# Attention values in fewer, longer bursts, and the room in SBUF that this takes

## The chip, the cores and the metric

The kernel runs on one core of one Trainium2 chip. The metric is the device time of one execution in microseconds (us). Before the change the median of three runs is 1562.35 us (1560.28 to 1562.48).

The core's engines work side by side, each through its own instructions in order: TensorE (PE in the profile, its weight loads PEld), VectorE (DVE), ScalarE (ACT), GpSimd (POOL), and SyncE (SP), which here issues nearly all DMAs. An instruction waits for semaphores that others raise; what stands behind it on the same engine waits with it.

## The reference

Eight batches of 1024 tokens with 256 features go through one gated block. Cut to what matters:

```python
xn = layernorm(x)                                  # no learned scale
q, k, v = split(xn @ W_attn + b_attn, 3)           # 16 heads of 16
q, k = rope(q), rope(k)                            # see below
att = softmax(where(causal, q @ k.T / sqrt(16), -inf))
s = (att @ v) @ W_proj + b_proj
h = silu(xn @ (w_gate / 127).T) * (xn @ (w_up / 127).T)   # 768 hidden, integer weights
g = silu(h @ (w_down / 127).T)
out = x + s * g
```

(The angles of rope depend on the head here and not on the token, so the kernel folds them into the weights once.)

## The kernel before

**Groups and halves.** The 16 heads of a batch form four groups of four, so there are 32 groups in all. A group works through its queries in two halves of 512. For half 0 there are four blocks of 128 keys, for half 1 eight: twelve *steps* n = 0 to 11 (`weight_steps`, L551). A step on the diagonal needs fewer queries: n = 0 to 3 have 512, 384, 256 and 128 columns, n = 4 to 7 have 512, and n = 8 to 11 again 512, 384, 256 and 128.

**One step.** `weights` (L554) makes the exponentials for one pair of heads: PE multiplies k by q into a PSUM tile `pw` (two of them, L564), ACT takes the exponential into a tile `e` in SBUF (L571), and on the diagonal POOL zeroes what lies above it (`affine_select`, L578). A step has two pairs, hence two `e` tiles. They come from the pool `pe` of six tiles, all of 2 x 512 columns whatever the step needs, used in turn. `values` (L592) multiplies v by these exponentials and adds up in the PSUM tile `av` (L600): four matmuls for the four heads, each with 32 columns of weights out of `v_sb`, side by side in the array; in fp32 each leaves two rows in the profile. v has a column of ones behind each head's 16, which makes the softmax's sum. After the last step of a half ACT copies `av` (L610), and `finish` (L613) transposes it on PE (`py`, L618) and divides on DVE.

**When values are added.** `attention` (L662) appends each finished step to `waiting`. As soon as three steps wait, `add_values(2)` (L694) does the oldest two: a *burst* of eight matmuls. The newest step always stays behind. The bursts come at the ends of steps n = 0, 2, 4, 6, 8 and 10. What `values` returns at the end of a half goes to `endings` and is called in the second pair of the next step (L683).

**The softmax's maxima.** They belong to the next group: while one group makes its weights, PE also multiplies q by k for the next group into `pm` (three PSUM tiles, L506), and DVE reduces each to row maxima (`top_far` L515, `top` L517). Their split high and low parts go through `shift_queries` (L539: transpose on PE, copy to `rows` on ACT, two DMAs on SP) into two extra rows of `q_st`, so the matmul of the weights subtracts them.

**Everything else** (projections, feed-forward, output) is cut into pieces in one long list, `chain`. `slot` (L822) is called after each bank of weights and each batch of maxima, and runs pieces so that PE's estimated work is spread evenly over a batch. The pieces use two PSUM tiles ("fill"). DVE's part of a piece is put off in `later` and issued by the next `flush`. The chain of a batch holds its feed-forward, the last batch's output and the next batch's q, k and v. The next batch's v comes last, while group 3 of the present batch runs.

**Projection of q and k** (`project_qk`, L230). PE makes `pqk` from two pieces; ACT writes `high`, a copy rounded to the matmul's reduced precision (L248), DVE writes `low`, the rest (L251), and SP sends both to DRAM (L256). `load` (L479) fetches a group's q and k from there, four DMAs each. `high` and `low` come from pool `p2`, which holds two tiles of each tag, while `p1` holds one. A tile that is used again waits until the DMA out of it has landed.

**Projection of v** (`project_v`, L263). Two token tiles at a time go to `pv`; DVE adds the bias on the way into `v_sb` (L278). There are two full `v_sb`, used by batches in turn.

**The opening.** Up to about 41 us the first batch is normalized, q and k for groups 0 and 1 are made by a Batch object called `opening`, and the weights are prepared. Then `forward` runs the maxima of group 0 with nothing to lie beside (L794): one chain piece for every two units, and among them the loads of group 1, `shift_queries(0)` for group 0 and the four remaining q/k projections of batch 0. The first weights follow.

Of the kernel before, what the change touches and what calls it, by code (L numbers as in the profile page):

```python
# [9 lines left out]
F32 = mybir.dt.float32  # L10
F32R = mybir.dt.float32r
# [3 lines left out]
ALU = mybir.AluOpType  # L15
AX = mybir.AxisListType

P = 128
HEADS = 16
HD = 16  # L20
SLOT = 32
# [14 lines left out]
def gated_block_kernel(ctx: ExitStack, tc: tile.TileContext, x, wqk, bqk, wv, bv, wp, bp, wg, wu, wd, rope, out):  # L36
# [139 lines left out]
    most = const.tile([P, 4], F32, name="most")  # L176
    flag = const.tile([1, 1], I32, name="flag")

    vs = [const.tile([P, NT, HEADS * VS + SLOT - VS], F32, name=f"v_sb_{i}") for i in range(2)]

# [11 lines left out]
        for j in which:  # L192
            engine.memset(stacks[i][j][half][PARTS:, :, :].bitcast(F32), (0.0, -1.0)[j])

    def set_ones(engine, i):
        whole = vs[i][:, :, : HEADS * VS].rearrange("p t (h s) -> p t h s", s=VS)
        engine.memset(whole[:, :, :, HD], 1.0)
        engine.memset(vs[i][:, :, HEADS * VS :], 0.0)

    p1 = ctx.enter_context(tc.tile_pool(name="p1", bufs=1))  # L200
    p2 = ctx.enter_context(tc.tile_pool(name="p2", bufs=2))
    pe = ctx.enter_context(tc.tile_pool(name="pe", bufs=6))


    QU = S // 4
# [2 lines left out]
    class Batch:  # L208
        def __init__(self, b, exact):
            self.b = b  # L210


            self.exact = exact
            self.hs = {}
# [15 lines left out]
        def project_qk(self, n, which, half, c):  # L230
            b = self.b
            i = which * (QK // 2 // P) + n
            if c == 0:
                self.pt = fill_tile("pqk")
            pt = self.pt
            nc.tensor.matmul(  # L236
                pt,
                wqk_sb[:, c, ts(i, P)],
                xnT[:, c, ts(half, HALF)],
                start=(c == 0),  # L240
                stop=(c == CC - 1),
            )
# [5 lines left out]
            nc.scalar.activation(high, pt, AF.Identity, bias=bqk_sb[:, i : i + 1])  # L248

            def rest():  # L250
                nc.vector.scalar_tensor_tensor(  # L251
                    low, pt, bqk_sb[:, i : i + 1], high.bitcast(F32), ALU.add, ALU.subtract
                )
                self.projected.add((n, which, half))
                for part, t in enumerate((high, low)):
                    nc.sync.dma_start(  # L256
                        out=qks[b % 2][which, part, ts(n, P // HD), :, ts(half, HALF)].rearrange("h d s -> (h d) s"),
                        in_=t.bitcast(F32),
                    )

            later.append(rest)

        def project_v(self, t):  # L263
            b = self.b
            if t % 2 == 0:
                self.pt = fill_tile("pv")
            pt = self.pt.rearrange("p (t d) -> p t d", t=2)
            for c in range(CC):
                nc.tensor.matmul(  # L269
                    pt[:, t % 2, :],  # L270
                    xnT[:, c, ts(t, P)],
                    wv_sb[:, c, :],
                    start=(c == 0),
                    stop=(c == CC - 1),
                )
            if t % 2:
                later.append(
                    lambda: nc.vector.tensor_tensor(  # L278
                        vs[b % 2][:, t - 1 : t + 1, : HEADS * VS].rearrange("p t (h s) -> p t h s", s=VS)[:, :, :, :HD],
                        pt.rearrange("p t (h d) -> p t h d", d=HD),  # L280
                        bv_sb.rearrange("p (h d) -> p h d", d=HD)[:, None, :, :].to_broadcast([P, 2, HEADS, HD]),
                        ALU.add,
                    )
                )

        def project_in(self):

# [180 lines left out]
    class Group:  # L468
# [85 lines left out]
        def weights(self, half, kb, pair):  # L554

            lo = max(0, kb * P - half * HALF)
            n = HALF - lo
            e = pe.tile([P, 2, HALF], F32, tag="e", name=f"e_{self.name}_{half}_{kb}_{pair}")

            def bank(first, count):  # L560
                pw = ps_pw.tile([P, HALF], F32, tag="pw", name=f"pw_{self.name}_{half}_{kb}_{pair}_{first}")
                for i in range(count):
                    head = 2 * pair + first + i
                    nc.tensor.matmul(  # L564
                        pw[:, ts(i, n)],
                        self.k_st[kb // QT][:, head, ts(kb % QT, P)],
                        self.q_st[half][:, head, lo:],
                        start=True,
                        stop=True,
                    )  # L570
                nc.scalar.activation(  # L571
                    e[:, first : first + count, lo:],
                    pw[:, : count * n].rearrange("p (a n) -> p a n", n=n),
                    AF.Exp,
                )
                if first + count == 2 and kb * P >= half * HALF:

                    nc.gpsimd.affine_select(  # L578
                        out=e[:, :, lo : lo + P],
                        in_=e[:, :, lo : lo + P],  # L580
                        pattern=[[0, 2], [1, P]],
                        compare_op=ALU.is_ge,
                        fill=0.0,
                        base=0,
                        channel_multiplier=-1,
                    )

            if 2 * n <= HALF:
                return e, [lambda: bank(0, 2), None]
            return e, [lambda: bank(0, 1), lambda: bank(1, 1)]  # L590

        def values(self, half, kb, es):  # L592
# [3 lines left out]
            if kb == 0:  # L596
                self.av = ps_av.tile([P, HALF], F32, tag="av", name=f"av_{self.name}_{half}")
            for j in range(4):
                at = (4 * self.g + j) * VS
                nc.tensor.matmul(  # L600
                    self.av[ts(j, SLOT), lo:],
                    vs[self.batch.b % 2][:, kb, at : at + SLOT],
                    es[j // 2][:, j % 2, lo:],
                    start=(kb == 0),
                    stop=(kb == last),
                )
# [20 lines left out]
            self.batch.complete[half] += 1  # L627

    STEPS = 3 * QT

    waiting, endings = [], []

# [29 lines left out]
    def attention(groups, at, plan, slot, vector):  # L662
# [5 lines left out]
        for n, (half, kb) in enumerate(group.weight_steps()):  # L668
            es = []
            for pair in range(2):  # L670
                e, banks = group.weights(half, kb, pair)
                es.append(e)
                for second, bank in enumerate(banks):
# [180 lines left out]
    with tc.tile_pool(name="setup", bufs=1) as sp:  # L854
# [21 lines left out]
        for i in range(2):  # L876
            set_ones(nc.gpsimd, i)

# [120 lines left out]
```

## Time and profile before

| what | value |
|---|---|
| median of the runs | 1562.35 us |
| profiled execution | 1562.15 us |
| its span, first to last instruction | 1560.4 us |
| granted TensorE clock over the span | 0.99 |
| `av` matmuls, L600 | 3072 rows, 290.8 us busy |
| `e`, L571 on ACT | 1280, 678.2 us busy |
| `high`, L248 on ACT | 64, 0.69 us each |
| bias add of v, L278 on DVE | 32, 0.69 us each |

The profile is of one execution and gives each instruction's start, length and releaser. Starts on PE are firm, while ends of matmuls are modelled and overlap, so PE's time is read from one start to the next. A granted clock of 1 is full speed. "Idle before, released by" names what an engine waited for; "issue" means nothing that the profile shows.

### The profile page before, as it was taken

To read this page: it belongs to the slowest core of one execution; us is meant where nothing else is said; L and a number is where in the kernel's file an instruction comes from. 1 tells how busy PE (TensorE), PEld (TensorE's weight loads), DVE (VectorE), ACT (ScalarE), POOL (GpSimd) and SP (SyncE) were. 2 spreads that over 40 slices of the span, in tenths; PEclk is the share of its full clock that TensorE was granted. 3 is DMA by queue.
4 is the path that set the end of the run, shared out by engine and by line. 5 is a ranking of instruction groups with operands and counts; after the bars stand their busy time and mean duration, and the time that the engine had idled before them with its cause. 6 is when DMAs were issued, how large, how long until landed. Compare 5 with 4: busy or idle time off the path is not lost.

```text
span 1560.4 us, 29514 instructions
## 1 busy us (share of the span) xinstructions
PE 1505.3 (96%) x9793; PEld 1058.2 (68%) x9793; DVE 1090.7 (70%) x3294; ACT 958.6 (61%) x2076; POOL 732.4 (47%) x1435
## 2 busy tenths in 40 slices
PE   4899999999999999999999999999999999999997
PEld 2577667776677766776667766777667776666664
DVE  8876776767767677776677766776776767767642
ACT  2266665676657666566655766667665766656664
POOL 4354443554436444464435734365343644434353
PEclk9899999999999999999999999999999999999999
DMA  7812544434554254543345344444455415445301
GB/s 186 185 29 42 109 104 63 96 54 104 102 103 68 49 110 96 102 76 69 91 81 112 60 96 96 74 97 63 96 110 94 78 36 123 88 70 83 49 15 44
DMA packets 86082, 132.86 MB, mean 85 GB/s; under 512 B 13856, under 2 KB 33824, under 8 KB 85920
## 3 DMA queue, kind: packets, MB, share of 16 engines
q1 hardware_dynamic: 85632, 130.60, 42.9%
q8 instruction: 80, 1.31, 0.4%
q14 instruction: 82, 0.67, 0.2%
q10 hardware_dynamic: 288, 0.27, 0.1%
HBM read 87.83 MB, written 41.94 MB: 83 GB/s over the span
## 4 chain that ended last, share of the span: by engine, by line
PE 85%; DVE 6%; ACT 2%; DMA 1%; POOL 1%; issue 1%; SPq 0%; ACTq 0%; DVEq 0%; POOLq 0%
PE pw L564 20%; PE av L600 17%; PE pm L506 16%; PE ph L327 10%; PE pqk L236 6%; PE pd L381 6%; PE pv L269 3%; PE po L434 3%; DVE top_far L515 2%; PE py L618 2%; DVE trash L517 1%; ACT e L571 1%; PE pyt L419 1%; DVE st L104 1%; PE pxt L224 1%
## 5 line engine op out<-in xcount | busy, mean ns | idle before, releaser
L571 ACT ACTIVATE e<-pw 128x512 f32<-128x512 f32 (+2 forms) x1280 | 678.2, 558 | 418.2 <-PE pw L564 393.5
L517 DVE CUSTOM_DVE_ANT_0 trash<-pm,mask_q 128x128 bf16<-128x128 f32 (+3 forms) x1024 | 500.6, 489 | 314.9 <-PE pm L506 276.7
L564 PE MATMUL pw<-q_st,k_st 67*128 67x512 f32 (+3 forms) x1536 | 548.2, 390 | 8.7 <-ACT e L571 5.4
L506 PE MATMUL pm<-k_st,q_st 65*128 65x512 f32 (+3 forms) x1536 | 529.3, 383 | 5.7 <-DMA qk<-high 1.7
L564 PEld LDWEIGHTS pw<-q_st,k_st 67*128 67x128 f32 x1536 | 282.0, 189 | 204.0 <-issue 92.9
L578 POOL TENSOR_SCALAR_AFFINE_SELECT e<-e 128x256 f32<-128x256 f32 x512 | 206.2, 408 | 412.0 <-ACT e L571 410.6
L515 DVE TENSOR_REDUCE top_far<-pm 128x1 f32<-128x512 f32 x512 | 336.7, 683 | 57.4 <-PE pm L506 56.7
L506 PEld LDWEIGHTS pm<-k_st,q_st 65*128 65x128 f32 x1536 | 279.4, 191 | 68.8 <-DVE top L517 17.0
L600 PE MATMUL av<-e,v_sb 128*32 128x512 f32 (+3 forms) x3072 | 290.8, 496 | 0.3 <-POOL e L578 0.3
L358 POOL TENSOR_TENSOR th<-th,ups 128x256 f32<-128x256 f32 x192 | 140.5, 732 | 232.7 <-DVE th L354 227.5
L600 PEld LDWEIGHTS av<-e,v_sb 128*32 128x32 f32 x3072 | 80.8, 109 | 133.0 <-issue 100.1
L362 POOL TENSOR_TENSOR h_low<-th,h_high 128x256 fp32r<-128x256 f32 x192 | 140.6, 732 | 15.4
L236 PE MATMUL pqk<-xnT,wqk_sb 128*128 128x512 f32 x256 | 133.7, 607 | 0.0
L327 PE MATMUL ph<-xnT_high,wg_sb 128*128 128x256 f32 x384 | 100.7, 284 | 0.0
L381 PE MATMUL pd<-wd_sb,h_high 128*128 128x256 f32 x384 | 98.0, 284 | 2.8 <-POOL h_high L361 2.8
L327 PE MATMUL ph<-xnT_high,wu_sb 128*128 128x256 f32 x384 | 100.5, 283 | 0.0
L327 PE MATMUL ph<-xnT_low,wu_sb 128*128 128x256 f32 x384 | 99.7, 282 | 0.0
L339 ACT ACTIVATE th<-ph 128x256 f32<-128x256 f32 x192 | 73.7, 384 | 42.2 <-PE ph L327 36.5
L327 PE MATMUL ph<-xnT_low,wg_sb 128*128 128x256 f32 x384 | 99.6, 282 | 0.0
L381 PE MATMUL pd<-wd_sb,h_low 128*128 128x256 f32 x384 | 97.2, 282 | 1.3 <-POOL h_low L362 1.3
L354 DVE SCALAR_TENSOR_TENSOR th<-th,ph 128x256 f32<-128x256 f32 x192 | 79.5, 414 | 18.6 <-ACT ups L343 17.1
L517 DVE DVE_READ_ACCUMULATOR2_ANT top<- 128x1 f32 x1024 | 84.6, 83 | 0.0
(93 smaller groups left out, 1668.2 us busy)
## 6 DMA issues: line engine op xcount, KB each, us to landing
q_st<-qk SPq DMA_DIRECT2D x256, 128.0 KB, 4.0
k_st<-qk SPq DMA_DIRECT2D x256, 128.0 KB, 5.2
qk<-high SPq DMA_DIRECT2D x64, 256.0 KB, 2.6
qk<-low SPq DMA_DIRECT2D x64, 256.0 KB, 2.8
xs<-in_x SPq DMA_DIRECT2D x16, 512.0 KB, 8.0
res<-in_x SPq DMA_DIRECT2D x32, 256.0 KB, 4.8
out<-res SPq DMA_DIRECT2D x32, 256.0 KB, 2.6
q_st<-rows SPq DMA_DIRECT2D x128, 8.0 KB, 1.9
```

The costliest lines, as they stand in the source:

```text
L236: nc.tensor.matmul(pt, wqk_sb[:, c, ts(i, P)], xnT[:, c, ts(half, HALF)], start=(c == 0), stop=(c == CC - 1),)
L327: nc.tensor.matmul(pt, self.weights[up][:, c, ts(hc, P)], part[:, c, ts(quarter, QU)], start=(c == 0 and i == 0), stop=(c == CC - 1 and i ...
L358: nc.gpsimd.tensor_tensor(h, th, ups, ALU.mult)
L362: nc.gpsimd.tensor_tensor(low, th, high.bitcast(F32), ALU.subtract)
L381: nc.tensor.matmul(pt, h[:, ts(i, P)], self.weights[2][:, hc, :], start=(hc == 0 and n == 0), stop=(hc == HC - 1 and n == len(hs) - 1),)
L506: nc.tensor.matmul(pm[:, ts(i, n)], self.q_st[half][:SHIFT, head, at], self.k_st[keys][:SHIFT, head, :n], start=True, stop=True,)
L515: nc.vector.tensor_reduce(self.top_far[:, head, qt - QT : qt - QT + 1], pm, AX.X, ALU.max)
L517: nc.vector.tensor_tensor_reduce(trash[:, :n], pm[:, ts(i, n)], mask_q[:, HALF - n :], 1.0, MASKED, ALU.add, ALU.max, self.top[:, head, qt ...
L564: nc.tensor.matmul(pw[:, ts(i, n)], self.k_st[kb // QT][:, head, ts(kb % QT, P)], self.q_st[half][:, head, lo:], start=True, stop=True,)
L571: nc.scalar.activation(e[:, first : first + count, lo:], pw[:, : count * n].rearrange("p (a n) -> p a n", n=n), AF.Exp,)
L578: nc.gpsimd.affine_select(out=e[:, :, lo : lo + P], in_=e[:, :, lo : lo + P], pattern=[[0, 2], [1, P]], compare_op=ALU.is_ge, fill=0.0, ba ...
L600: nc.tensor.matmul(self.av[ts(j, SLOT), lo:], vs[self.batch.b % 2][:, kb, at : at + SLOT], es[j // 2][:, j % 2, lo:], start=(kb == 0), sto ...
```

## The change

- **Bursts.** `add_values` no longer follows a count of three. It is called in step n = 0, 4 and 7 of each group (`BEHIND`), between the two pairs, and does all that waits: at n=0 the last group's steps 7 to 11 (five), at n=4 steps 0 to 3 (four), at n=7 steps 4 to 6 (three). `endings` are called in the first pair of a step instead of the second.
- **Weights' room.** `pe` has seven tiles instead of six. Steps of 256 and 128 columns use narrow tiles of their own from `p2` instead, two of each width.
- **v.** Columns of groups 0 to 2 are held once (`v_most`), those of group 3 twice (`v_last`, batches in turn). The bias add of v becomes two instructions.
- **High and low.** `project_qk` takes them from `p1`, one tile of each, instead of two. The `opening` takes both out of one weights' tile.

```diff
-    vs = [const.tile([P, NT, HEADS * VS + SLOT - VS], F32, name=f"v_sb_{i}") for i in range(2)]
+    LAST = HEADS - 4
+    v_most = const.tile([P, NT, LAST * VS + SLOT - VS], F32, name="v_most")
+    v_last = [const.tile([P, NT, 4 * VS + SLOT - VS], F32, name=f"v_last_{i}") for i in range(2)]
...
-    def set_ones(engine, i):
-        whole = vs[i][:, :, : HEADS * VS].rearrange("p t (h s) -> p t h s", s=VS)
-        engine.memset(whole[:, :, :, HD], 1.0)
-        engine.memset(vs[i][:, :, HEADS * VS :], 0.0)
+    def set_ones(engine):
+        for v_sb, heads in ((v_most, LAST), (v_last[0], 4), (v_last[1], 4)):
+            whole = v_sb[:, :, : heads * VS].rearrange("p t (h s) -> p t h s", s=VS)
+            engine.memset(whole[:, :, :, HD], 1.0)
+            engine.memset(v_sb[:, :, heads * VS :], 0.0)
...
-    pe = ctx.enter_context(tc.tile_pool(name="pe", bufs=6))
+    pe = ctx.enter_context(tc.tile_pool(name="pe", bufs=7))
...
-            high, low = (
-                p2.tile([P, HALF], F32R, tag=part, name=f"{part}_{b}_{i}_{half}") for part in ("high", "low")
-            )
+            if self.parts_room:
+                room = self.parts_room.tile([P, 2, HALF], F32, tag="e", name=f"parts_{b}_{i}_{half}").bitcast(F32R)
+                high, low = room[:, 0], room[:, 1]
+            else:
+                high, low = (
+                    p1.tile([P, HALF], F32R, tag=part, name=f"{part}_{b}_{i}_{half}") for part in ("high", "low")
+                )
...
-                later.append(
-                    lambda: nc.vector.tensor_tensor(
-                        vs[b % 2][:, t - 1 : t + 1, : HEADS * VS].rearrange("p t (h s) -> p t h s", s=VS)[:, :, :, :HD],
...
+                def rest():
+                    for v_sb, first, heads in ((v_most, 0, LAST), (v_last[b % 2], LAST, 4)):
+                        of = slice(first * HD, (first + heads) * HD)
+                        nc.vector.tensor_tensor(
+                            v_sb[:, t - 1 : t + 1, : heads * VS].rearrange("p t (h s) -> p t h s", s=VS)[:, :, :, :HD],
...
-            e = pe.tile([P, 2, HALF], F32, tag="e", name=f"e_{self.name}_{half}_{kb}_{pair}")
+            name = f"e_{self.name}_{half}_{kb}_{pair}"
+            if 2 * n > HALF:
+                e = pe.tile([P, 2, HALF], F32, tag="e", name=name)[:, :, lo:]
+            else:
+                e = p2.tile([P, 2, n], F32, tag=f"e_{n}", name=name)
...
-                at = (4 * self.g + j) * VS
+                head = 4 * self.g + j
+                v_sb, at = (v_most, head) if head < LAST else (v_last[self.batch.b % 2], head - LAST)
                 nc.tensor.matmul(
                     self.av[ts(j, SLOT), lo:],
-                    vs[self.batch.b % 2][:, kb, at : at + SLOT],
-                    es[j // 2][:, j % 2, lo:],
+                    v_sb[:, kb, at * VS : at * VS + SLOT],
+                    es[j // 2][:, j % 2, :],
...
+    BEHIND = (0, QT, 2 * QT - 1)
...
-                    if pair == 1 and second and endings:
+                    if pair == 0 and second and endings:
                         endings.pop(0)()
...
                 if vector:
                     vector.pop(0)()
+                if pair == 0 and n in BEHIND:
+                    add_values(len(waiting))
             waiting.append((group, half, kb, es))
-            if len(waiting) == 3:
-                add_values(2)
...
         opening = Batch(0, None)
+        opening.parts_room = pe
```

More of the change, by code (lines that the diff above doesn't have):

```diff
@@ L213, in __init__ @@
             self.exact = exact
+            self.parts_room = None
             self.hs = {}
@@ L276, in project_v @@
             if t % 2:
-                later.append(
-                    lambda: nc.vector.tensor_tensor(
-                        vs[b % 2][:, t - 1 : t + 1, : HEADS * VS].rearrange("p t (h s) -> p t h s", s=VS)[:, :, :, :HD],
[L280 to L284, printed above, removed]
+                def rest():
[3 more added lines that the diff above has]
+                            v_sb[:, t - 1 : t + 1, : heads * VS].rearrange("p t (h s) -> p t h s", s=VS)[:, :, :, :HD],
+                            pt[:, :, of].rearrange("p t (h d) -> p t h d", d=HD),
+                            bv_sb[:, of].rearrange("p (h d) -> p h d", d=HD)[:, None].to_broadcast([P, 2, heads, HD]),
+                            ALU.add,
+                        )
+                later.append(rest)
         def project_in(self):
@@ L571, in bank @@
                 nc.scalar.activation(
-                    e[:, first : first + count, lo:],
+                    e[:, first : first + count, :],
                     pw[:, : count * n].rearrange("p (a n) -> p a n", n=n),
@@ L578, in bank @@
                     nc.gpsimd.affine_select(
-                        out=e[:, :, lo : lo + P],
-                        in_=e[:, :, lo : lo + P],
+                        out=e[:, :, :P],
+                        in_=e[:, :, :P],
                         pattern=[[0, 2], [1, P]],
@@ L875, in gated_block_kernel @@
         set_rows(nc.gpsimd, 0, 1, [1])
-        for i in range(2):
-            set_ones(nc.gpsimd, i)
+        set_ones(nc.gpsimd)
         def turn(src, dst, n, even, odd):
```

## The prediction

> **What bounds the kernel now.** I read the page's engine table and its 40 slices first, then its chain. PE is busy 96% of the span, the slices show it at 9 from second to last but one, and the chain runs on PE for 85%. So PE's order of work sets the time between about 74 us (the first weights) and the last group, and what PE loses between its instructions counts in full there.
>
> ```profile
> PE 1505.3 (96%) x9793; PEld 1058.2 (68%) x9793; DVE 1090.7 (70%) x3294; ACT 958.6 (61%) x2076; POOL 732.4 (47%) x1435
> PE   4899999999999999999999999999999999999997
> PE 85%; DVE 6%; ACT 2%; DMA 1%; POOL 1%; issue 1%; SPq 0%; ACTq 0%; DVEq 0%; POOLq 0%
> ```
>
> Busy PE is not PE at its best. The list of waits has PE's weight load idle before `av`, released by nothing but "issue", far more than any other wait of PE:
>
> ```profile
> PEld av L600 <- issue: 100.1, 336, 0.8
> PEld pw L564 <- ACT e L571: 69.9, 211, 1.0
> PEld pm L506 <- DVE top L517: 17.0, 54, 0.7
> ```
>
> The timeline of PE in the middle of the kernel shows what this costs in PE's time. The columns are start, length, engine and line; lengths overlap, so I read differences of starts.
>
> ```profile
> 715.53 0.34 PE L506 MATMUL pm<-k_st,q_st 65*128 65x384 f32 x1
> 715.80 1.92 PE L600 MATMUL av<-e,v_sb 128*32 128x512 f32 x16
> 717.65 0.44 PE L564 MATMUL pw<-q_st,k_st 67*128 67x384 f32 x1
> 717.93 0.34 PE L506 MATMUL pm<-k_st,q_st 65*128 65x384 f32 x1
> ...
> 718.83 0.34 PE L564 MATMUL pw<-q_st,k_st 67*128 67x384 f32 x1
> 719.01 0.34 PE L506 MATMUL pm<-k_st,q_st 65*128 65x384 f32 x1
> 719.18 0.34 PE L564 MATMUL pw<-q_st,k_st 67*128 67x384 f32 x1
> ...
> 723.99 1.71 PE L600 MATMUL av<-e,v_sb 128*32 128x512 f32 x16
> 725.63 0.44 PE L564 MATMUL pw<-q_st,k_st 67*128 67x128 f32 x2
> ```
>
> A 384-wide `pm` or `pw` takes 0.18 us to the next start (719.01 to 719.18). The last one before a burst of values takes 0.27 (715.53 to 715.80): 0.09 lost on entering. The first `pw` after it takes 0.28 (717.65 to 717.93): 0.10 lost on leaving. Ahead of `pw` of 128 columns that is 0.05. The burst itself: two steps of 512 columns take 1.85 us, 512 and 384 take 1.64, and 256 and 128 (another place of the trace) 0.79. So 640 columns make 1.06 us, 1.66 ns each, and 0.15 us is left over that doesn't grow with columns. Inside, four waves (two a step) start 0.45, 0.43 and 0.43 us apart and reach the next `pw` after 0.54, at 512 columns; 0.24, 0.22, 0.11 and 0.22 at 256 and 128. Only the first and the last wave take longer than their columns. One burst thus costs 0.34 us beyond its columns, 0.29 before a narrow `pw`. Over all 192 bursts the starts repeat to within 0.01 us in their medians.
>
> **The bursts: 192 become 96.** Before, a group has six bursts of two steps, two of them ahead of narrow `pw`: 4 x 0.34 + 2 x 0.29 = 1.94 us. Now it has three, of four steps (n=4), three (n=7) and five (n=0 of the next group), all ahead of a 512-wide `pw`: 3 x 0.34 = 1.02. The 1536 matmuls and their columns stay. Saved 0.92 x 32 = **29 us**, all on PE's path. [...] But inner waves go exactly with their columns (0.43, 0.22, 0.11), so loads hide there, and the loss is one of a burst's ends. I go by the trace. Ends: 27 to 30 us.
>
> **Room for weights.** With seven wide tiles in turn, tile k waits for tile k-7. Counting through a group (16 wide tiles), every such tile has been freed by an earlier burst, or by the burst directly ahead on PE (second pair of n=0 and of n=7), which precedes the pair's own `pw` anyway. Narrow tiles of n=2, 3 are freed at n=4, those of n=10, 11 at n=0. No wait of ACT is added: 0. The last step's `affine_select` on POOL (0.41) now has half a step less of lead, but comes last in a burst of 2.1 to 3 us: 0.
>
> **v in three tiles.** The add of 512 elements (0.69) becomes 384 and 128. By DVE rows of 512 (0.69) and 256 (0.42) elements those are 0.55 and 0.29: +0.15, 32 times, 5 us of DVE. 28 lie under DVE's 30% of idle time; two in the opening's DVE-bound stretch cost 0.3, two before it at most 0.3: **0.6 us**; all 5 if that cover were gone. v's pieces of the next batch come after its last q/k pieces, well into group 3, while group 2's last values come at n=0 of group 3: the single tile makes no wait. Two more memsets (0.25 each) lie under POOL's 3.5 us wait for `raw`. The opening's high and low in weight tiles: ACT waited for no landing there before, so 0.
>
> **high and low once instead of twice.** Now each `high` (L248) waits for the landing of the one before it. In steady work a landing comes before the next `high` or `low` in batches 1 to 7, mostly by 3 us or more and at the least by 0.1, and up to n=4 bursts shift both alike; only one in batch 0 falls short, by 0.65. I take **1 us** (0 to 7: one 1 us miss per batch). In the opening it is otherwise:
>
> ```profile
> 47.09 0.69 ACT L248 ACTIVATE high<-pqk,bqk_sb 128x512 fp32r<-128x512 f32 x1 [4.05 <-PE pqk L236]
> 49.89 0.69 ACT L248 ACTIVATE high<-pqk,bqk_sb 128x512 fp32r<-128x512 f32 x1 [2.12 <-DMA k_st<-qk]
> 54.16 0.69 ACT L248 ACTIVATE high<-pqk,bqk_sb 128x512 fp32r<-128x512 f32 x1 [3.58 <-DMA qk<-high]
> 56.61 0.69 ACT L248 ACTIVATE high<-pqk,bqk_sb 128x512 fp32r<-128x512 f32 x1 [1.76 <-PE pqk L236]
> ...
> 51.42 0.75 DVE L251 SCALAR_TENSOR_TENSOR low<-pqk,bqk_sb,high 128x512 fp32r<-128x512 f32 x1
> 58.55 0.74 DVE L251 SCALAR_TENSOR_TENSOR low<-pqk,bqk_sb,high 128x512 fp32r<-128x512 f32 x1
> ```
>
> The first landing is at 54.05 (it held the third `high` there). Now it holds the second, until 54.8. DVE has its `low` next at 51.42, and behind that the maxima, which hold PE's three `pm` tiles: DVE, idle nowhere from 48 to 75, loses 3.4 us. The second part lands by about 57, in time for the third. That third one's issue on SP stands behind eight loads of q and k, which now start near 56. In mid-kernel (405 us) eight such loads with a `high` behind them took 10.9 us from the first issue to `high`'s landing, so it lands near 66.9, the fourth `high` ends at 67.6, and DVE's fourth `low`, due at 58.55 + 3.4, waits 5.7 us more. Together 9.1 on DVE, with `rows` (ACT) and PE's next `pm` queued behind. PE reached its first `pw` at 73.2 and sat 0.9 us for the rows' landing; the rows now land near 76, so that wait goes: **+8.5 us** (3 if DVE makes up the second wait, 10 if loads crowd).
>
> **What longer stretches cost.** A burst lets ACT and DVE catch up. Summed over PE's starts, time over the usual start-to-start is 6% of PE's time in the first us after a burst and 9 to 14% in the five after it, not rising towards the end. With 96 fewer first microseconds, 96 x 0.05 = **4.5 us** more stalls (-2 to 12). In the last group about 3.5 us of values move behind its steps 8 to 10, where ACT is near its limit: **0.5** (0 to 2). `finish` follows its burst by one step, as before, so its 0.44 us of `py` and DVE's 0.68 move without a wait.
>
> **Sum**, against the profiled execution (1562.15 us: span 1560.4 and 1.75 around it; the median of the runs is 0.2 above it): 1562.15 - 29 + 8.5 + 0.6 + 1 + 4.5 + 0.5 = 1548.3, so **1548**. With half of each term's distance to its ends added up, this case alone spans 1541 to 1556.
>
> **Rivals.**
> *Starved engines (slower).* At a burst DVE has at most three `pm` tiles, 2.1 us of work. Bursts up to 1.85 us leave it none idle; those of 2.1, 2.6 and 3.0 leave it 1.4 us a group. DVE has 32.5 us of work per group of 46.4; outside bursts that is (32.5 - 8.6)/37.8 = 63% now and (32.5 - 6.3)/37.5 = 70% then. If stalls go as load/(1-load), they grow by 37%; those above 0.14 us sum to 83 us, so +31 instead of +4.5: 1575. It decides from +18 us, 0.6 us a group. For it: `pw` has but two tiles, and burst-free stretches grow from 6 us to 11 to 15. Against: the stall share above doesn't rise with the time since a burst.
> *The opening hides the single buffer.* If the third part's landing isn't late, only the first 3.4 us or nothing is lost: 1540 to 1543. For it: landings vary from 2.0 to 7.8 us. Against: DVE has no idle time there.
> *The loss goes with steps, not bursts*[...]: no gain, 1577. Against it stand the inner waves, which show no loss at the step from one to the next.
>
> **Chances.** The sum 0.56; opening hidden 0.18; partly starved (5 to 18 us more, 1553 to 1562) 0.11; starved 0.11; loss by steps 0.04. About 0.2% (3 us) is what a measurement of this kernel can tell from no change. Faster: 0.56 + 0.18 + most of partly starved 0.09 = 0.83; the same 0.05; slower 0.12. The range for 8 in 10 takes in the hidden opening and partial starving: 1538 to 1562.
>
> **What would show it.** Right: 96 bursts; the weight load's idle before `av` near half of 100 us; groups about 45.6 us instead of 46.4; the first `pw` near 82 instead of 74 us, behind two waits of `high` for a landing. Wrong: a first `pw` at 74 to 78 (opening hidden), or more idle time of PE's loads behind `e` (69.9) and `top` (17.0), by over 20 us (starved), or more ns per column in long bursts.

## The result and the profile after

The changed kernel takes 1579.86 us (median of five runs, 1577.53 to 1580.85), where the kernel before takes 1562.35. The ratio is 1.0109, with a 95% interval of 1.0094 to 1.0124: 1.1% slower. The forecast was 1548, with a range of 1538 to 1562, so both the time and its sign were wrong.

The profiled execution took 1580.84 us with a span of 1579.1, 18.7 us more span than before. The lines of the page that answer to those shown of before, and the granted clock beneath them (40 slices of 39.5 us):

```profile
PE 1506.5 (95%) x9793; PEld 1078.9 (68%) x9793; DVE 1092.0 (69%) x3326; ACT 954.0 (60%) x2076; POOL 731.2 (46%) x1437
PE   4789999999999999999999999999999999999997
PEclk9799999989999999989999999998999999999999
PE 80%; ACT 6%; POOL 4%; DVE 3%; issue 2%; DMA 0%; SPq 0%; POOLq 0%; DVEq 0%; ACTq 0%
```

PE is still busy in 95% of the span and still bounds the kernel. Two things are new. The clock row has an 8 in three slices in mid-kernel, where before had none. And the chain of the last end gives 4% to POOL and 6% to ACT, against 1% and 2% before. The waits of PE and of its feeders (engine, operation, line, released by: total us, count, longest):

```profile
PEld av L617 <- issue: 125.9, 440, 0.7
PEld pw L580 <- ACT e L587: 73.8, 224, 0.8
PEld pm L518 <- DVE top L529: 24.8, 70, 2.6
ACT high L256 <- DMA qk<-high: 15.9, 3, 9.0
PE pm L518 <- ACT yT L437: 10.7, 6, 1.8
ACT xs L135 <- POOL newton L126: 8.7, 6, 1.5
```

The last three lines lead to where the time went. ACT's `high` waits three times for a landing, all in the opening. PE waits six times for `yT`, a copy on ACT, and ACT waits six times for `newton` on POOL: once in each of batches 1 to 6. The first line did not fall although the bursts were halved; that is taken up below.

**The opening.** ACT's timeline (start, length, line, idle before and its releaser):

```profile
53.14 0.69 ACT L256 ACTIVATE high<-pqk,bqk_sb 128x512 fp32r<-128x512 f32 x1 [4.74 <-DMA qk<-high]
55.99 0.69 ACT L256 ACTIVATE high<-pqk,bqk_sb 128x512 fp32r<-128x512 f32 x1 [2.16 <-DMA qk<-high]
65.68 0.69 ACT L256 ACTIVATE high<-pqk,bqk_sb 128x512 fp32r<-128x512 f32 x1 [9.00 <-DMA qk<-high]
```

Each `high` now waits for the one before to land, as forecast, and the first `pw` comes at 81.92 us instead of 74.25: 7.7 us of the 18.7.

**The steps.** From the first `pw` to the last row of PE the time went from 1478.6 to 1489.6 us, 11.0 more, where the forecast had 22 less. Groups 4, 8, ... 24, the first of each later batch, take 48.4 to 49.8 us and three of their successors about 50, where the others of these batches take 45.4 to 45.9 (before: 46.7 or 46.8 for the first of a batch, 46.2 to 46.8 for the rest). The place is the same in all six, at step n = 11. Here it is in group 4, PE's timeline first:

```profile
313.00 0.40 PE L518 MATMUL pm<-k_st,q_st 65*128 65x512 f32 x1
313.24 0.33 PE L580 MATMUL pw<-q_st,k_st 67*128 67x128 f32 x2
315.35 0.50 PE L518 MATMUL pm<-k_st,q_st 65*128 65x512 f32 x1 [1.78 <-ACT yT L437]
```

ACT's at the same time:

```profile
311.91 0.38 ACT L355 ACTIVATE ups<-ph 128x256 f32<-128x256 f32 x1
313.74 0.60 ACT L135 ACTIVATE xs<-xs,newton,rstd 128x256 f32<-128x256 f32 x1 [1.45 <-POOL newton L126]
314.24 0.58 ACT L587 ACTIVATE e<-pw 128x512 f32<-128x512 f32 x1
314.72 0.58 ACT L437 COPY yT<-pyt 128x512 f32<-128x512 f32 x1
```

And POOL's:

```profile
309.18 1.29 POOL L460 TENSOR_TENSOR o<-o,gate 128x512 f32<-128x512 f32 x1 [1.02 <-DVE o L457]
310.55 1.30 POOL L461 TENSOR_TENSOR res<-res,o 128x512 f32<-128x512 f32 x1
...
313.47 0.23 POOL L126 TENSOR_SCALAR newton<-newton 128x8 f32<-128x8 f32 x1
```

`xs` is the first scaling of the next batch's x; its bias is `newton`, the last of the short operations by which POOL works out mean and variance. They stand behind two operations of 1.3 us. ACT comes to `xs` 1.45 us too early, and behind `xs` stand the exponentials and the copy `yT`, whose PSUM tile `pyt` holds one of the three `pm` tiles. PE stands still for 1.78 us. In the kernel before the same pair just fitted (timeline, POOL then ACT):

```profile
303.86 0.23 POOL L126 TENSOR_SCALAR newton<-newton 128x8 f32<-128x8 f32 x1
304.52 0.60 ACT L135 ACTIVATE xs<-xs,newton,rstd 128x256 f32<-128x256 f32 x1
```

POOL was done at 304.09, 0.4 us before ACT asked. What lay in this stretch was the burst that used to end n = 8. PE before, then PE after, from the same piece `po` on (rows in between left out):

```profile
296.96 1.03 PE L434 MATMUL po<-wp_sb,yT 128*128 128x256 f32 x4
...
298.09 1.92 PE L600 MATMUL av<-e,v_sb 128*32 128x512 f32 x16
...
304.20 0.60 PE L419 MATMUL pyt<-ident,y 128*128 128x128 f32 x4
```

```profile
306.69 1.03 PE L446 MATMUL po<-wp_sb,yT 128*128 128x256 f32 x4
...
311.85 0.60 PE L431 MATMUL pyt<-ident,y 128*128 128x128 f32 x4
```

Counted from this `po`, POOL has `newton` after 7.1 us before and 7.0 after, so it lost nothing. ACT comes for it after 7.6 us before and 5.6 after: 2 us sooner, which is the burst of 1.85 us with its ends. (The burst that used to end n = 10 begins at 305.68, behind this place. It hid no wait of ACT, but it was work for PE while ACT waits; run 7 shows what that is worth.)

The stall has a second cost. Windows of this trace (us; busy time of PE, PEld, DVE, ACT, POOL with counts; granted clock; share and GB/s of DMA) from group 4's steps over the stall and on:

```profile
268.90:316.90 48.00, 45.62 (x314) 34.10 (x312) 35.12 (x115) 28.42 (x62) 24.87 (x54) 1.00 0.53 100
316.90:327.10 10.20, 10.20 (x48) 5.29 (x50) 4.01 (x15) 3.16 (x7) 7.49 (x13) 0.50 0.74 104
327.10:367.80 40.70, 40.46 (x296) 32.05 (x288) 28.49 (x84) 28.96 (x67) 17.32 (x35) 1.00 0.19 34
```

About 1.6 us after the stall PE gets half its clock for 10.2 us, and does 48 matmul rows in them. The same 10.2 us follow in groups 12 and 20, from 692.4 and 1067.9 us; in the other three batches nothing follows (the last section says which stalls these are). With half clock the two groups that share these 10.2 us take 49.1 and 50.0 us (4 and 5), 49.6 and 49.5 (12 and 13), 49.8 and 49.3 (20 and 21); without it 48.4 and 45.8 (8 and 9). That is 4.9 us more for each such pair of groups.

### The profile page after: what moved, and what is told of

Read it like the earlier page. It is cut to its first block, busy times and chain, and to the rows that moved or that the text cites. A ratio compares the mean times of both kernels' runs of the same rounds, so it can differ in the third digit from the quotient of the medians.

```text
span 1579.1 us, 29394 instructions
## 1 busy us (share of the span) xinstructions
PE 1506.5 (95%) x9793; PEld 1078.9 (68%) x9793; DVE 1092.0 (69%) x3326; ACT 954.0 (60%) x2076; POOL 731.2 (46%) x1437
## 4 chain that ended last, share of the span: by engine, by line
PE 80%; ACT 6%; POOL 4%; DVE 3%; issue 2%; DMA 0%; SPq 0%; POOLq 0%; DVEq 0%; ACTq 0%
PE pw L580 18%; PE av L617 17%; PE pm L518 16%; PE ph L339 9%; PE pqk L240 6%; PE pd L393 5%; PE po L446 3%; ACT e L587 3%; PE pv L277 3%; PE py L635 2%; DVE trash L529 1%; DVE top_far L527 1%; POOL th L370 1%; POOL e L594 1%; ACT high L256 1%
## 5 line engine op out<-in xcount | busy, mean ns | idle before, releaser
L518 PE MATMUL pm<-k_st,q_st 65*128 65x512 f32 (+3 forms) x1536 | 536.8, 388 | 22.3 <-ACT yT L437 10.7
L580 PEld LDWEIGHTS pw<-q_st,k_st 67*128 67x128 f32 x1536 | 288.1, 191 | 151.7 <-ACT e L587 73.8
L518 PEld LDWEIGHTS pm<-k_st,q_st 65*128 65x128 f32 x1536 | 283.7, 193 | 92.1 <-DVE top L529 24.8
L617 PE MATMUL av<-e,v_most 128*32 128x512 f32 (+3 forms) x2304 | 209.0, 505 | 0.0
L617 PEld LDWEIGHTS av<-e,v_most 128*32 128x32 f32 x2304 | 68.8, 112 | 121.7 <-issue 93.5
L374 POOL TENSOR_TENSOR h_low<-th,h_high 128x256 fp32r<-128x256 f32 x192 | 140.7, 733 | 15.4
L240 PE MATMUL pqk<-xnT,wqk_sb 128*128 128x512 f32 x256 | 137.0, 622 | 0.0
L627 ACT COPY avs<-av 128x512 f32<-128x512 f32 x64 | 37.5, 586 | 162.5 <-PE av L617 162.5
L351 ACT ACTIVATE th<-ph 128x256 f32<-128x256 f32 x192 | 73.7, 384 | 49.3 <-PE ph L339 38.2
```

The source lines that it names most:

```text
L240: nc.tensor.matmul(pt, wqk_sb[:, c, ts(i, P)], xnT[:, c, ts(half, HALF)], start=(c == 0), stop=(c == CC - 1),)
L374: nc.gpsimd.tensor_tensor(low, th, high.bitcast(F32), ALU.subtract)
L518: nc.tensor.matmul(pm[:, ts(i, n)], self.q_st[half][:SHIFT, head, at], self.k_st[keys][:SHIFT, head, :n], start=True, stop=True,)
L580: nc.tensor.matmul(pw[:, ts(i, n)], self.k_st[kb // QT][:, head, ts(kb % QT, P)], self.q_st[half][:, head, lo:], start=True, stop=True,)
L617: nc.tensor.matmul(self.av[ts(j, SLOT), lo:], v_sb[:, kb, at * VS : at * VS + SLOT], es[j // 2][:, j % 2, :], start=(kb == 0), stop=(kb == ...
```

## The experiments

Two causes stood beside each other after this reading: the room (single `high` and `low`) and the bursts, these by the new wait or by starved engines. The first four runs separate them. Bursts and endings were moved by one change, and no run separates these two; "the bursts" stands for both below. In all that follows "first `pw`" is its start on PE, and ratios are against the kernel before.

**1. The stall alone.** Two more empty places in the list of chain pieces put the scaling of x later behind POOL's `newton`.

```diff
-            *([offset, lambda: None] if b else []),
+            *([offset, *[lambda: None] * 3] if b else []),
```

> The changed kernel with one edit: between the last step of the next batch's normalization on POOL (newton) and ACT's first scaling of x stand three empty places instead of one, so ACT comes to that scaling one step later. Theory (one stall, doubled by the clock): in the first group of six batches ACT stands behind newton, yT and PE's pm behind ACT, PE idles 1.8 us, and in three of them the granted clock falls to half for 10.2 us right after; without the wait both go: 6 x 1.9 = 11 us and 3 x 4.9 = 15 us, so about 1554. Rival (starved engines: long stretches between bursts make ACT and DVE the limit everywhere): that wait is a symptom, another takes its place, 1577 to 1580. Rival (the half clock comes from the long bursts themselves, not from the stall): only the stall goes, 1568, with three half-clock stretches left.

Measured: 1555.74 us (1552.26 to 1556.46), ratio 0.9936 (0.9914 to 0.9958). Two list entries are worth 24 us. The same windows of this run:

```profile
268.90:316.90 48.00, 47.40 (x324) 35.82 (x323) 36.53 (x120) 28.16 (x62) 24.66 (x53) 1.00 0.51 100
316.90:327.10 10.20, 10.20 (x88) 7.67 (x88) 6.66 (x28) 7.24 (x17) 9.76 (x19) 1.00 0.68 104
```

The 10.2 us now hold 88 rows at full clock instead of 48, and no group from 4 to 27 has a stretch of half clock. Group 4 takes 46.4 us (49.1), group 5 45.8 (50.0). So the wait of `xs` for `newton`, with the clock behind it, is the largest part of the loss. Its two parts are much alike: six stalls of 48.4 - 46.4 = 2.0 us make 12, three stretches of half clock at 4.9 make 15. They add to 27; the medians differ by 24, those of the kernel before beside them by 2 (1562.35 and 1564.33).

**2. The room in the opening.** Batch 0's remaining projections take `high` and `low` out of weight tiles, as `opening` does, so that none waits for a landing.

```diff
+        batches[0].parts_room = pe
         first = groups[0]
...
         first.shift_parts(1)
+        batches[0].parts_room = None
```

> The changed kernel with one edit: the four q/k projections of batch 0 that run among the maxima of the opening take high and low out of weights' tiles too, as the opening's own do, so none waits for the landing of the one before it. Theory: the first pw comes back from 81.9 to about 74.3 us, and the time falls by 7 to 8 us, to about 1572; all else stays. Rival (the later first pw comes from v's split add or from the memsets, not from high): no change, 1579.

Measured: 1576.28 us (1573.55 to 1583.33), ratio 1.0069 (1.0045 to 1.0092); first `pw` at 74.1 instead of 81.9. That is the opening's 7.8 us back. The median gains only 3.6. The stalls of n = 11 remain, and the clock's answer to them varies: the slowest of the four executions, 1583.33 us, has the lowest mean clock, 0.973, and the fastest, 1573.55, has 0.980. That slowest one is the profiled one. It has half clock for 10.2 us behind the stalls of groups 4, 8 and 20 and for 3.4 behind that of group 16. It has 20.5 us more of it in group 28, in stretches of 3.4 and 17.1, where no standstill of PE over 0.2 us precedes.

**3. The bursts of two back, all else as changed.**

```diff
-                if pair == 0 and n in BEHIND:
-                    add_values(len(waiting))
             waiting.append((group, half, kb, es))
+            if len(waiting) == 3:
+                add_values(2)
...
-                    if pair == 0 and second and endings:
+                    if pair == 1 and second and endings:
```

> The changed kernel with the bursts alone undone: two steps at the end of every second step, endings in the second pair again. Kept are seven wide tiles, narrow tiles, v in three tiles, one high and one low. Theory: the room costs only the opening, first pw at about 82, PE's stall behind newton and the half clock after it are not there, 192 bursts again: 1570 to 1572. Rival (the room itself, v's single tile or high's single tile, stalls steady work): 1575 or more, with groups over 46.8 us. Starved engines would also have 1570 here, since its stretches are short.

Measured: 1569.4 us (1566.46 to 1572.09), ratio 1.0043 (1.0029 to 1.0057). First `pw` at 81.1, groups of 46.7, 46.7, 46.1 and 46.2 as before, no half clock from group 1 to the last, and a span of 1564.7, 4.3 above before's. Seven tiles, narrow tiles, v in three parts and single `high` and `low` cost the steps nothing; they cost the opening. And with the bursts back in their places there is no stall at n = 11: their move is what uncovered it.

**4. Both mends** (edits 1 and 2 together).

> The changed kernel with both edits of the two runs before: ACT's scaling later, and high and low of the opening's four projections out of weights' tiles. Theory: 1579.9 - 26 - 7.5 = 1546, below the kernel before by 1%, with the bursts' saving of 28 us less some 12 us of other stalls. Starved engines: 1570 to 1573. Half clock from the bursts themselves: 1560.

Measured: 1548.5 us (1547.51 to 1548.81), ratio 0.9896 (0.9877 to 0.9914). First `pw` at 75.3, groups of 46.4 to 45.5, the last group 51.8 (49.9 before).

**5. Both mends with bursts of two** (edits 1 to 3 together): what do the longer bursts bring without the room's cost and the stall?

> The changed kernel with both mends and with bursts of two steps at the ends of steps, so that against the run with both mends (1548.5) only the bursts differ. Theory: room and mends together cost and bring nothing, 1561 to 1564, first pw near 74; the bursts alone are then worth 13 to 15 us, half of the 29 that their ends cost. Rival (the later scaling of x is itself a gain, whatever the bursts): 1555 or less.

Measured: 1561.66 us (1558.54 to 1563.45), ratio 0.9987 (0.9977 to 0.9997). So the longer bursts bring 1561.66 - 1548.5 = 13.2 us net (15.4 from the first `pw` to PE's last row in the two traces), not the 24.5 of the forecast (29 less 4.5). To see where the rest went I took PE's start-to-start times in all groups of both traces and sorted what differs into three heaps. The usual time of the ordinary rows, the same in both, is left out; "usual" is what a row of that kind and width mostly takes:

| us over all groups | bursts of two | long bursts | difference |
|---|---|---|---|
| rows of `av`, and what the row before and the row after a burst take beyond the usual | 314.3 | 284.0 | -30.3 |
| stalls: what other rows of `pm`, `pw`, `ph`, `pd` take beyond the usual, where that is over 0.05 us | 128.3 | 151.3 | +23.0 |
| all other rows | 201.3 | 195.3 | -6.0 |

The first row has the forecast's 29. The stalls take back 23, or 17 with the last row. What is taken as usual moves each of these by some us, but not their differences' signs. By releaser the largest growth is behind ACT's `e`, 31.9 to 43.9 us; behind DVE it is 15.1 to 15.6.

The length of the stretches doesn't explain the growth. Take groups 4 to 27, where neither trace has half clock, the median as the usual, and the time since the last burst. In the first 6 us after a burst these stalls take 9.1% of PE's time with bursts of two, and 13.1% with long bursts; further from a burst than that, where nearly only the long stretches reach, they take 8.4%. So they grew right behind the new bursts. By step they grew most at n = 1, from 12.2 to 19.4 us. Long bursts differ from those of two here in three things: their length, their place between the pairs, and the endings, which are now called in the first pair. With both mends, long bursts and the endings back in the second pair, the program waits for itself for ever, so there is no time for that case. Run 6 bears on the length; place and endings stay open.

The burst itself costs what its columns said. Both traces at PE, first the longest kind in the mended kernel, five steps, and the `pw` behind it:

```profile
402.43 3.22 PE L617 MATMUL av<-e,v_most 128*32 128x512 f32 x40
405.58 0.50 PE L580 MATMUL pw<-q_st,k_st 67*128 67x512 f32 x1
```

That is 3.15 us; the forecast's 1.66 ns a column over 512 + 512 + 384 + 256 + 128 columns and 0.15 for the ends make 3.12. The waits of the load engine before `av`, on the other hand, point the wrong way; those before `pw` go with the bursts. With 96 bursts:

```profile
PEld av L617 <- issue: 117.2, 430, 0.7
PEld pw L580 <- issue: 54.8, 159, 0.8
PEld av L617 <- POOL e L594: 5.7, 23, 0.3
```

With 192:

```profile
PEld av L617 <- issue: 96.9, 329, 0.8
PEld pw L580 <- issue: 92.4, 180, 1.2
PEld av L617 <- POOL e L594: 14.4, 44, 0.8
```

More "issue" before `av` with half the bursts, though PE loses 30 us less: this idle time doesn't measure what a burst loses. (That it lies largely inside bursts, where PE is fed, would explain it and is not shown.)

**6. Long bursts, or fewer?** Both mends, with six bursts a group in mid-step, and then with four.

```diff
-    BEHIND = (0, QT, 2 * QT - 1)
+    BEHIND = range(0, STEPS, 2)
```

> The changed kernel with both mends, and one size changed: values added at n = 0, 2, 4, 6, 8, 10, between the pairs, so 192 bursts again instead of 96, each of two steps; room, mends and all else as in the run with both mends (1548.5). Theory (each burst costs 0.3 us at its ends, and half of that saving is lost again to waits in the longer stretches between bursts): PE's burst rows and their neighbours grow by 29 us, stalls elsewhere fall by 15 to 20, so 1558 to 1564. Rival (bursts' ends cost nothing net): 1548. Rival (longer stretches cost nothing): 1577.

Measured: 1583.88 us (1583.83 to 1584.66), ratio 1.0133 (1.0116 to 1.015), far above what was expected. The stalls between bursts did fall, by 14.4 us, but the rows of the bursts rose by 49.6. Of the fall some 6 us lie ahead of group 0's first burst, where the clock differs between the two traces. In groups 4 to 27 (median as the usual) the stalls are 74.5 us with bursts of two at the ends of steps, 91.7 with long bursts and 86.3 here, and n = 1 has 19.8: short stretches alone give back less than a third of the growth. The waits say why the bursts' rows rose:

```profile
PEld av L617 <- POOL e L594: 33.4, 73, 1.8
PE av L617 <- POOL e L594: 6.2, 12, 1.5
```

A mid-step burst of two holds, as its last step, the one just made, whose triangle POOL is still clearing. In a burst of three to five steps that step comes last, 1.7 to 2.8 us after the burst's start, and POOL is done by then: the forecast put the cost at 0 for three bursts, rightly (5.7 us in run 4). Here this cover is gone. The ends of 96 more bursts at 0.29 to 0.34 us make 28 to 33 of the 49.6; the rest goes with these waits, 33.4 and 6.2 us.

```diff
-    BEHIND = (0, QT, 2 * QT - 1)
+    BEHIND = (0, 2, QT, 2 * QT - 1)
```

> As the run before, with values added at n = 0, 2, 4 and 7: 128 bursts, the four-step burst cut into two of two steps. Theory: 32 more bursts cost 9 to 11 us, the shorter stretch behind n=0 gives back 2 to 6: 1552 to 1557. If the lost part of the saving sits in the stretch from n=0 to n=4 alone, 1548 or less; if it sits elsewhere, 1558.

Measured: 1563.73 us (1559.67 to 1566.79), ratio 1.0005 (0.9995 to 1.0016), above what was expected. The 32 added bursts cost 19.7 us in their rows (0.6 each, twice the ends' price) and give back 3.4 us of stalls; the last group is 3.3 us longer. The load's wait for POOL's `e` before `av`, 18.3 us against 5.7, has a part in it. An early burst of two does not buy the stalls back.

**7. Does a wait alone do it, in the kernel before?** First the kernel before without its empty place, so that ACT asks for `newton` sooner.

```diff
-            *([offset, lambda: None] if b else []),
+            *([offset] if b else []),
```

> The kernel before with one edit: no empty place between newton on POOL and ACT's first scaling, so ACT comes to it about 2 us earlier, where its lead over POOL's end was 0.4 us. Its bursts stay at two steps. Theory [...]: PE stalls in the first group of six batches, 1 to 1.5 us each, with half-clock stretches in some of them, 1568 to 1582. Rival (only the new bursts bring the clock down): the stalls alone, 1567 to 1570, no half clock in groups 4 to 27. If two pw tiles hide ACT's wait: 1562.

Measured: 1561.59 us (1559.54 to 1565.94), ratio 0.9995 (0.9984 to 1.0006). Then POOL was held up behind `newton` by 10 multiplications by one, and by 18:

```diff
             nc.gpsimd.tensor_scalar(newton, newton, -1.0, None, ALU.mult)
+            for _ in range(10):
+                nc.gpsimd.tensor_scalar(newton, newton, 1.0, None, ALU.mult)
```

> The kernel before, bursts of two steps untouched, with ten more small POOL operations (newton times 1, some 0.28 us apart) between newton and its use, about 2.8 us, so that ACT, which had 0.4 us in hand, waits about 2.4 us with yT and the weights behind it, once in each of seven batches. Theory ([...]the length of bursts doesn't matter): PE stalls 1.5 to 2 us in six or seven batches, 9 to 14 us, and half-clock stretches of some us follow some of them, 1572 to 1595 in all. Rival (the half clock needs the new long bursts): stalls only, 1570 to 1576, and no half clock in groups 4 to 27.

> As the run before with eighteen such operations, about 5 us, so that ACT waits some 4.6 us. Theory: PE stalls near 4 us in six or seven batches (24 to 28 us), and half clock follows all of them, up to 5 us each: 1600 to 1625. Rival: the stalls alone, 1586 to 1590.

Measured: with 10, 1574.05 us (1573.52 to 1574.17), ratio 1.0074 (1.0057 to 1.009); with 18, 1601.48 (1599.38 to 1604.58), ratio 1.0257 (1.0238 to 1.0276). ACT's wait in the three runs, in this order (total, count, longest):

```profile
ACT xs L135 <- POOL newton L126: 6.2, 7, 0.9
```

```profile
ACT xs L137 <- POOL newton L128: 16.0, 6, 2.7
```

```profile
ACT xs L137 <- POOL newton L128: 31.1, 6, 5.2
```

A wait of 0.9 us is absorbed. One of 2.7 is longer than the changed kernel's 1.45, yet PE has the burst of n = 10 to do meanwhile: group 4 takes 1.1 us more and the clock stays full in groups 4 to 27. (More than half of the 12 us lies elsewhere: group 0 is 7.6 us longer, where the feed-forward waits for POOL.) So the first run was inconclusive on the clock, and the second shows how much a burst at this place hides. One of 5.2 us outlasts that burst. PE's timeline and the clock's windows there:

```profile
311.90 1.70 PE L602 MATMUL av<-e,v_sb 128*32 128x512 f32 x12
316.41 1.49 PE L602 MATMUL av<-e,v_sb 128*32 128x384 f32 x4 [2.82 <-POOL e L580]
```

```profile
316.40:323.00 6.60, 6.59 (x21) 4.71 (x22) 1.61 (x4) 4.09 (x10) 5.27 (x11) 0.54 0.00 1
323.00:360.00 37.00, 36.74 (x273) 27.95 (x272) 26.01 (x84) 26.58 (x60) 20.00 (x37) 1.00 0.43 66
```

With bursts of two, too, the clock is halved at such a standstill of 2.8 us, in all six batches: for 6.8 us in this one, where it begins at 315.6 within the standstill, and for 3.4 in the others. So the standstill is enough, without long bursts.

**8. One burst at the end of its step.** Both mends, and the burst of n = 4 after the step's second pair instead of between the pairs.

```diff
-                if pair == 0 and n in BEHIND:
+                if pair == (n == QT) and n in BEHIND:
```

> The run with both mends (1548.5), with the four-step burst of n=4 moved behind the second pair of its step; seven tiles suffice for that. The bursts' number and sizes stay. Theory (part of the saving was lost because a burst between a step's pairs leaves the next step crowded: PE's stalls at n=5 were 13 us there and 8 with bursts at a step's end): 3 to 6 us less, 1543 to 1546. Rival (it is the number of bursts that counts, not their place in a step): 1548 to 1550.

Measured: 1543.14 us (1542.62 to 1544.8), ratio 0.988 (0.9864 to 0.9897): the fastest of all, 1.2% below before. The reason named for it did not show: stalls went from 151.3 to 150.5 us in all (n = 5 down from 13.1 to 10.4, n = 4 up from 8.5 to 11.2). Of the span's 5.8 us, 1.8 are an earlier first `pw` (73.4), which this edit doesn't explain, and 2.1 less in `av` rows; the rest is spread. So the expected time came about, and not by the expected way. Why `av` rows fell wasn't tried.

## Why the prediction was wrong

The balance, from the differences that the runs give: the bursts' rows -30, stalls behind the new bursts +17, the opening +7.7, the wait for `newton` with the clock behind it +24. They add to the span's change, +18.7. That it fits so closely is in part luck: these are differences from several pairs of runs, and the median of the kernel before alone lay between 1562.0 and 1564.3.

- **"192 become 96", 29 us:** right. The rows of the bursts fell by 30.3, and a five-step burst costs its columns and one pair of ends. The rival "the loss goes with steps" falls with that: by it these rows would have kept their time.
- **Room for weights, v, POOL's `affine_select`: 0 to 1:** right for three bursts (runs 3 and 5 for room and v, run 4 for the select). With bursts of two in mid-step (run 6) the select's cover is gone.
- **"high and low once", +8.5 in the opening:** right in mechanism and size, +7.7. The two waits of `high` that it names are there, 4.74 and 9.00 us; a third of 2.16 us between them, where it had the landing in time, is not in the forecast. In steady work the 1 us was not seen.
- **"What longer stretches cost", +4.5 (-2 to 12): the first step that failed.** It measured 17. (The product in it, 96 x 0.05, is 4.8; that changes nothing.) The forecast took the share of PE's time that is lost after a burst from the kernel before and carried it over. That the share doesn't rise further out was right: 8.4% beyond 6 us, against 9.1% within 6 us with bursts of two. What failed is that it stays the same within these 6 us: behind the new bursts it is 13.1%. The forecast gave their new place between the pairs and the moved endings nothing there. Which of these two it is stays open; that the stretches are longer makes less than a third of it (run 6). The rival "starved engines" had the sign and half the distance, but neither its engine (DVE; the growth is behind ACT's `e`) nor its reason (burst-free stretches), and at 17 it stays below the 18 from which it would have decided. That its 1575 lies near the measured 1580 is luck, for it has no stall at n = 11. This step alone would have left a gain.
- **The step that wasn't there: what the removed bursts covered for other queues.** The one at the end of n = 8 held ACT up by 2 us, so POOL had finished `newton` when ACT came for it, with 0.4 us in hand. The forecast asked of each *changed* operation what covers it (the select, the add of v, `finish`) and of the removed bursts only what they cost. It never asked which waits of ACT on POOL ended just in time beside them. The forecast has no term for it. With the halved clock that it set off it is 24 us, more than the whole net gain of bursts, and turned the sign.
- **The last group, +0.5:** 49.9 became 51.8, so nearer to 2.
- **"What would show it":** 96 bursts and the first `pw` came true; groups of about 45.6 nearly (45.9 in the mean with both mends). "The load's idle before `av` near half of 100" was a bad sign to watch: it rose to 125.9 while the loss it was to stand for fell. The reading behind it, that this wait is by far PE's longest, passed over another line of the same view of before:

```profile
PEld pw L564 <- issue: 92.9, 182, 1.4
```

This one did fall, to 54.4 in the changed kernel.

## What to carry to other kernels

A block of work that is moved off a place was also cover there. Before costing it by its own time alone, list the waits of the *other* engines that ended within a microsecond of their need beside it; here 0.4 us in hand between POOL and ACT was worth 24 us. And a share of stalls that was read behind short bursts at the ends of steps holds for those: behind bursts of another length and place it has to be measured again, or the range must allow for it (here 17 us instead of 4.5).

## What the runs showed of the hardware

A standstill of TensorE in mid-kernel can cost more than its length. After 1.78 us without a matmul, in otherwise dense work, the granted clock of the changed kernel fell to 0.5 for 10.2 us in three places of six; in run 2, which has the same stalls, for 10.2, 10.2, 3.4 and 10.2 us in four of six. At 2.8 us (run 7, 18 multiplications) it fell in six of six, for 3.4 to 6.8 us. In the groups 4 to 27 of runs 1 and 3, where PE stood still for less than 0.7 us at a time, it never fell. Nor did it in the kernel before from 122.74 to 1409.57 us, where PE's longest standstill is 0.63 us.

Which stalls are followed by half clock goes with a grid in time. A trace holds the time of each change of the granted clock. In those of the kernel before and of the changed kernel, every stretch from one change to the next is a whole number of times 3.413 us, to within 0.002 us: 3.413, 6.827, 10.240 or 13.653 us at half clock, and at full clock, to take one, 365.226 us from 327.17 to 692.39 in the changed kernel, 107 times 3.413. The changed kernel's six stalls on its grid:

| stall of PE (us) | length | lines of the grid | granted clock after it |
|---|---|---|---|
| 313.57 to 315.35 | 1.78 | whole between 313.51 and 316.93 | 0.5 from 316.93 to 327.17 |
| 503.89 to 505.67 | 1.78 | cut by 504.66 | 1 |
| 689.47 to 691.25 | 1.78 | whole between 688.98 and 692.39 | 0.5 from 692.39 to 702.63 |
| 879.79 to 881.55 | 1.76 | cut by 880.13 | 1 |
| 1065.19 to 1066.97 | 1.78 | whole between 1064.45 and 1067.86 | 0.5 from 1067.86 to 1078.10 |
| 1255.57 to 1257.35 | 1.78 | cut by 1255.59 | 1 |

The clock fell at the end of the stretch in which a stall lies whole, and behind none that a line cuts, be it by 0.02 us. The six of run 2 went the same way: four whole and followed, two cut and not followed. The six of 2.8 us in run 7 have 2.05 us or more within one stretch, whatever the cut, and all were followed at its end. So where a stall fell on the grid was luck, and with it whether the run lost about 4.9 us more. It is no full rule: in the kernel before a standstill of 1.36 us (115.51 to 116.86, cut by 115.91) was followed by half clock from 119.33 to 122.74, and in the last group of the run with four bursts one of 1.55 us was followed although a line cuts it.

Nor does half clock come behind standstills alone: the kernel before has it for 3.4 us in group 28, from 1409.57 us, with no gap on PE over 0.2 us in the 10 us ahead of it, and run 2 its 3.4 and 17.1 us there. What else brings the clock down, no run here shows.
